# Score chunks in another order, first transposes earlier, norms spread out, last tile turned after one more half unit

## The chip, the cores and the metric

The kernel runs on one core of a Trainium2 chip. The metric is the device time of one execution, in microseconds. Inside a core TensorE (PE; weight loads are shown apart as PEld), VectorE (DVE), ScalarE (ACT) and GpSimd (POOL) each work through a queue of instructions in order and wait for each other through semaphores. SyncE (SP) issues most DMAs, in order; POOL and ACT issue some. SBUF is the on-chip memory, PSUM the banks that PE writes its products to.

## The reference

One transformer block on 2048 tokens of width 512, in float32: attention with 16 heads of 128, then a layer of 64 experts with 4 chosen for each token, plus shared experts.

```python
h = _layernorm(x) * (1 + ca) + sa
# attention, per head: q, k, v from h; causal softmax; out = sum over heads of attn @ O_w + O_b
logits = jnp.einsum('bqhd,bkhd->bhqk', q, k) / math.sqrt(d_head)
scores = jax.nn.softmax(jnp.where(causal_mask, NEG, logits), axis=-1)
out = jnp.einsum('bqhd,hdm->bqm', jnp.einsum('bhqk,bkhd->bqhd', scores, v), O_w) + O_b
x = x + ga * out
h = _layernorm(x) * (1 + cb) + sb
# router: softmax(h @ Wr + bias), top 4 of 64 experts, at most 128 tokens each
# experts: (silu(xb @ Wg) * (xb @ Wu)) @ Wd, weighted; shared experts: the same form on all tokens
x = x + gb * ffn(h)
```

`sa, ca, ga, sb, cb, gb` come from `silu(c) @ wmod`.

## The kernel before

The 2048 tokens are 16 tiles of 128. The order of the instructions is written by hand: the helper `merge` takes several streams of (cost, function) items and always emits the next item of the stream that is furthest behind by share of cost; *marks* are functions that are emitted when a given share of all cost is done. Within each engine instructions then run in the order in which they were emitted, apart from some products that are brought forward.

**Attention.** The query tiles are taken in pairs: pair `pr` is tiles 2pr and 2pr+1 (`i` = 0, 1). Causality gives tile qi a row of (qi+1)*128 columns of scores. A head is done in five steps s, with the pairs `BATCHES` = (7), (6), (5, 0), (4, 1), (3, 2). There are 80 steps (16 heads of five). In step n three things are merged: the softmax of step n+2, fillers (for s below 3 the projections of the next head's q and k by `project`, then the values of the next group of heads), and `weighted_values` of step n (scores times values, L644). The fourth thing is at the marks 0.58, 0.66, 0.8 and 0.88: the four transposes `turn(n + 1, a)` of step n+1.

A tile's row of scores is made in chunks of at most 1024 columns. For one chunk (`chunk`, in `softmax_tile`): PE writes the scores (L572) into one of **two** PSUM buffers `ps` (tag `sc`); DVE adds the causal mask to the last 128 columns (L584), finds the negated maximum (L585) and, for a second chunk, the minimum with the first (L589); ACT takes the exponential and the sum (L591) into `p`, and for a second chunk the factor `fix` (L601). When a tile has its last chunk, `normalise` is put on the list `left`; it is emitted inside the next chunk, or at the end of the step: L547 or L550 to L554 make the reciprocal sums. The scaling of `p` follows on ACT (L795) after the next chunk's exponential, or on DVE (L559) for tile 0 of the single pairs. A chunk's scores can start only when the exponential of the chunk two before has read its buffer.

At the end of each step `swap` issues 16 DMAs on SP (L616), 32 partitions by 32 columns blocks of `p` to `pt`; then DVE turns each of the four parts of `pt` in place (L626), and these are the right operands of L644. The four `turn`s of step 0 stand apart, ahead of the loop: steps 0 and 1 have their softmax before it, merged with the values of the first heads.

`project` makes seven products (L222) in two PSUM buffers of their own (tag `mm`): the first is read by ACT (L230), the second by DVE with the first's result (L236), the third by DVE (L240), the fourth by two (L248, L249), then L253, L257, L261.

`tiles_of(s)` gives the order of the tiles in a softmax step. Chunks of a tile are adjacent:

- (5, 0): (0,0) 128; (5,1) 1024, 512; (0,1) 256; (5,0) 1024, 384
- (4, 1): (4,1) 1024, 256; (1,1) 512; (4,0) 1024, 128; (1,0) 384
- (3, 2): (3,1) 1024; (2,1) 768; (3,0) 896; (2,0) 640

**Output tiles and routing.** The first `NE` = 4 output tiles have their first 15 heads done as fillers in attention's last steps; the last head is added at L1119 and L1126. Then `norm` is called for the four of them. `norm(t)` is seven instructions on DVE (L954 to L965), one square root on ACT (L958, before L959) and a DMA of h on POOL (L966). The tiles 4 to 15 follow, 16 heads of PE each (L1140). At places given by tables, `turn_h(t)` (four transposes on PE, L972, and a copy by ACT, L973), `logit(t)` (four products, L981), `choose`, `positions` and `seat_tokens` of earlier tiles are emitted between the heads: `turn_h(0)` after head 10 of tile 4, `logit(0)` after its head 14, `turn_h(1)` after head 0 of tile 5, `logit(1)` after its head 3. Two of PE's orders matter here: the buffer of the turned tile (tag `tr`) and the three instructions on ACT, root, copy and the exponential of `choose`, which share one queue.

**After the last tile** come the shared experts' first ten half units (`shared[:LEAD]`, eight PE instructions each, L1203; after two of them ACT and DVE make their gated product, L1191 to L1193), with the last tile's turn, seats, logit, choice and positions between them. Then the experts run, merged with the other shared units.

Of the kernel before, what the change touches and what calls it, by code (L numbers as in the profile page):

```python
# [23 lines left out]
def adaln_block_kernel(  # L24
# [24 lines left out]
    _, N, D = x.shape  # L49
    H, _, DH = Q_w.shape  # L50
    E, _, HE = Wg.shape
    S, _, HS = Sg.shape
# [68 lines left out]
    NE = 4  # L121
    parts = [silc.rearrange("p k n -> p (k n)")]
    with ExitStack() as att:
# [143 lines left out]
        with tc.tile_pool(name="pre", bufs=1) as pre, tc.manual_schedule():  # L267
# [4 lines left out]
            for b in range(NB):  # L272
# [5 lines left out]
                if b == 0:  # L278
                    wms = {}
                    for i in (1, 0):  # L280
                        wms[i] = pre.tile([P, DC, D], F32, name="wm", bufs=2)
                        nc.sync.dma_start(
                            out=wms[i],
# [233 lines left out]
                    return at  # L517
                at += 4 * o + 3

        def tiles_of(s):  # L520

            prs = BATCHES[s]
            if len(prs) == 1:
                return [(prs[0], 1), (prs[0], 0)]
            if prs[1] == 0:
                return [(0, 0), (prs[0], 1), (0, 1), (prs[0], 0)]
            return [(prs[0], 1), (prs[1], 1), (prs[0], 0), (prs[1], 0)]

        def softmax_tile(hd, s, pr, i, pb):

# [266 lines left out]
        probs = {}  # L797
        turned = {}

        def softmax_work(n):  # L800
            hd, s = steps[n]
            probs[n] = pp.tile([P, PW], F32, name="p")
            out = []
            for pr, i in tiles_of(s):
                out += softmax_tile(hd, s, pr, i, probs[n])
            return out

        def swap(n):
            flush()
# [3 lines left out]
        def turn(n, a):  # L813
            turn_blocks(steps[n][1], turned[n], a)

        with tc.manual_schedule():
            work = softmax_work(0) + softmax_work(1)
            fill = [(1024, lambda t=t: make_v(0, t)) for t in range(NT)]
            fill += [(2048, lambda j=j: plain(0, j, qts[0, j])) for j in (2, 0, 1)]
            merge([work[:4], fill[:8]], [])  # L820
            swap(0)
            merge([work[4:], fill[8:]], [])
            swap(1)
            for a in range(4):
                turn(0, a)
            outs = []
            for n, (hd, s) in enumerate(steps):
                if s == 3:
                    if hd + 2 < H:
                        heads[hd + 2] = load_head(hd + 2)  # L830
                    if hd % HG == 1 and hd // HG + 2 < NG:
                        groups[hd // HG + 2] = load_group(hd // HG + 2)
                fill = fillers(hd, s)
                if (hd, s) in MOD_LOADS:
                    load_mod(MOD_LOADS[hd, s], hd // HG)
                if (hd, s) in MOD_ROWS:
                    fill.append((2048, lambda m=MOD_ROWS[hd, s]: late_mod(*m)))
                if (hd, s) in ((2, 3), (15, 2)):
                    mag = qkw.tile([P, 512], F32, name="p_")
                    gate(mag, ga if hd == 2 else gb)  # L840
                if (hd, s) == (14, 0):
                    nc.sync.dma_start(out=sgb, in_=modd.partition_broadcast(P))
                if (hd, s) == (14, 1):
                    fill.insert(2, (0, lambda: load_wo(0)))
                if (hd, s) == (14, 2):
                    load_wo(1)
                    load_ab(0, heads=((0, 4), (4, 8)))
                if (hd, s) == (14, 3):
                    load_wo(2)
                    load_ab(0, heads=((8, 12), (12, 14)))  # L850
                    first, second = [
                        vow.tile([P, DC, HG, DH], F32, name="wv").rearrange("p k i d -> p (k i d)")
                        for _ in range(2)
                    ]
                    parts += [first[:, :D], first[:, D:], second[:, :D]]
                    last3 = second[:, D : D + (NE - 1) * P]
                if (hd, s) == (14, 4):
                    load_wo(3)
                    load_ab(0, heads=((14, 15),))
                    for u in range(NE):  # L860
                        load_x_tile(u)
                    rest = spare(hd // HG)
                    nc.sync.dma_start(out=rest[0][:, :D], in_=O_b.partition_broadcast(P))
                    for u in range(NE):
                        outs += begin_output(u)
                if hd == H - 1 and s == 0:
                    load_ab(1, heads=((0, 4), (4, 8)))
                if hd == H - 1 and s == 1:
                    load_ab(1, heads=((8, 12), (12, 15)))
                if hd == H - 1 and s == 2:  # L870
                    load_ab(2)
                if hd == H - 1 and s == 4:
                    nc.vector.tensor_copy(ga, rest[0][:, D:])
                    nc.sync.dma_start(out=last3, in_=atd[H - 1, :, : (NE - 1) * P])
                    nc.sync.dma_start(out=ones, in_=atd[H - 1, :, (NE - 1) * P : NE * P])
                if outs:
                    upto = 8 if hd < H - 1 else (14, 14, 14, 10)[s]
                    fill += outs[:upto]
                    del outs[:upto]
                streams = [fill, weighted_values(hd, s, turned.pop(n))]  # L880
                if n + 2 < len(steps):
                    streams.insert(0, softmax_work(n + 2))
                marks = [(f, lambda i=i: scale_wo(i)) for f, i in WO_SCALES.get((hd, s), ())]
                if s == 4 and hd + 2 < H:
                    marks.append((0.05, lambda: scale_w(hd + 2)))
                    marks.append((0.3, lambda: sum_w(hd + 2)))
                if n + 1 < len(steps):
                    for a, at in enumerate((0.58, 0.66, 0.8, 0.88)):
                        marks.append((at, lambda a=a: turn(n + 1, a)))
                merge([st for st in streams if st], marks)  # L890
                if n + 2 < len(steps):
                    swap(n + 2)
            assert not outs and not ahead
# [216 lines left out]
    with tc.manual_schedule():  # L1110
        load_x(1)
        load_ab(3, heads=ALL)
        load_ab(2, heads=((15, 16),))
        route_consts()
        for j in range(2, NB):
            load_x(j)
        for t in range(NE):
            ps = psO.tile([P, D], F32, name="pso", tag="y")
            nc.tensor.matmul(  # L1119
                out=ps,  # L1120
                lhsT=last3[:, t * P : (t + 1) * P] if t < NE - 1 else ones,
                rhs=wos[(H - 1) // 4][:, (H - 1) % 4, :],
                start=True,
                stop=True,
            )
            nc.vector.tensor_add(acc[:, t, :], parts[t], ps)  # L1126
        for t in range(NE):
            norm(t)
        for t in range(NE, NT):
            pr, i = divmod(t, 2)  # L1130
            if i == 0 and 3 <= pr < NP - 1:
                load_ab(pr + 1, heads=ALL)
            if i == 1 and pr >= NP - 1 - S:
                s = pr - (NP - 1 - S)
                if s < S:
                    nc.sync.dma_start(out=wsg[:, s], in_=Sg[s].rearrange("(k p) h -> p k h", p=P))
                    nc.sync.dma_start(out=wsu[:, s], in_=Su[s].rearrange("(k p) h -> p k h", p=P))
            ps = psO.tile([P, D], F32, name="pso", tag="y")
            for hd in range(H):
                nc.tensor.matmul(  # L1140
                    out=ps,
                    lhsT=abs_[pr][:, hd, i * P : (i + 1) * P],
                    rhs=wos[hd // 4][:, hd % 4, :],
                    start=(hd == 0),
                    stop=(hd == H - 1),
                )
                if hd == 5:
                    nc.vector.tensor_add(acc[:, t, :], acc[:, t, :], ga)
                if (t, hd) in TURN:
                    turn_h(TURN[t, hd])  # L1150
                if (t, hd) in POSITION:
                    positions(POSITION[t, hd])
                if (t, hd) in SEAT:
                    seat_tokens(SEAT[t, hd])
                if (t, hd) in LOGIT:
                    u = LOGIT[t, hd]
                    logit(u)
                    if u in LASTS:
                        for _ in choose(LASTS.index(u)):
                            pass  # L1160
            nc.vector.tensor_add(acc[:, t, :], acc[:, t, :], ps)
            norm(t)
# [3 lines left out]
    with ExitStack() as ex:  # L1166
# [214 lines left out]
        with tc.manual_schedule():  # L1381
# [3 lines left out]
                load_down(e)  # L1385
            for n, (_, f) in enumerate(shared[:LEAD]):
                f()
                if n == 1:
                    turn_h(NT - 1)
                if n == 2:  # L1390
                    seat_tokens(len(BLOCKS) - 2)
                if n == 2:
                    logit(NT - 1)
# [176 lines left out]
```

## Time and profile before

| | |
|---|---|
| runs, median (lowest to highest) | 2424.36 us (2423.91 to 2430.88) |
| the profiled execution | 2410.55 us, span 2408.8 |
| PE idle in the span (2408.8 - 2344.1) | 64.7 us |
| attention, start to the last weighted values | 54 to 1680 us |
| output tiles and routing | 1680 to 1884 us |
| shared first units | 1884 to about 1930 us |

A profile lists each engine's instructions by line of the kernel, with tiles as out<-in. "Idle before" is how long the engine stood still ahead of an instruction, and "<-" names what it waited for. The "granted clock" is the share of full speed that TensorE was given in a stretch. A matmul in float32 is issued as two instructions; 512 columns take 0.43 us each from start to start, 256 columns 0.215, although each is shown longer as they overlap. The 16 heads repeat with a period of about 97.5 us.

### The profile page before, as it was taken

How to read it: one execution, taken by the hardware profiler on the slowest of the kernel's cores; microseconds unless marked ns; L12 is line 12 of the kernel's file. 1: busy time of each engine (PE TensorE's matmuls, PEld its weight loads, DVE VectorE, ACT ScalarE, POOL GpSimd, SP SyncE). 2: the span in 40 equal slices, each digit the busy share in tenths (PEclk: the TensorE clock that was granted, in tenths of full speed). 3: DMA queues.
4: the chain of work that ended last, by engine and by line, in shares of the span. 5: the costliest groups of instructions: out<-in, count | busy, mean ns of one | idle time of the engine just before them, and what ended most of it. 6: DMA issues, size and time to landing. Idle time of an engine off the chain costs nothing.

```text
span 2408.8 us, 27742 instructions
## 1 busy us (share of the span) xinstructions
PE 2344.1 (97%) x9078; PEld 1503.7 (62%) x9078; DVE 1554.9 (65%) x3100; ACT 864.0 (36%) x1703; POOL 219.1 (9%) x286
## 2 busy tenths in 40 slices
PE   7999999999999999999999999999999999999999
PEld 3666656666576675766766656555444476876743
DVE  5367767677676776767767767764655563644664
ACT  3344444444444444444444444442211221222200
POOL 0000000000000000000000000000000111111074
PEclk9999999999999999999999999999999999999999
DMA  4234544354453444444535445675432368778665
GB/s 140 63 72 119 125 115 114 94 144 109 97 135 96 118 121 95 114 111 103 122 94 127 114 101 120 169 197 142 137 123 87 101 203 247 236 218 240 193 194 160
DMA packets 223835, 325.84 MB, mean 135 GB/s; under 512 B 31894, under 2 KB 138442, under 8 KB 223692
## 3 DMA queue, kind: packets, MB, share of 16 engines
q1 hardware_dynamic: 196812, 252.74, 40.8%
q0 software_dynamic: 17664, 54.54, 7.6%
q10 hardware_dynamic: 9216, 16.78, 1.9%
q8 instruction: 73, 1.20, 0.2%
q14 instruction: 70, 0.57, 0.1%
HBM read 139.39 MB, written 41.95 MB: 75 GB/s over the span
## 4 chain that ended last, share of the span: by engine, by line
PE 75%; SPq 7%; DVE 7%; issue 3%; DMA 3%; ACT 2%; POOL 1%; ACTq 0%; DVEq 0%
PE ps L572 14%; PE po L644 14%; PE pqk L222 14%; SPq L616 7%; PE pso L1140 6%; PE pst L1287 5%; PE pse L1432 5%; PE psd L1349 5%; PE pv L447 4%; DVE pt L626 3%; PE psy L1453 2%; PE psg L1203 2%; PE psb L769 2%; DVE nm L585 1%; PE tpx L1425 1%
## 5 line engine op out<-in xcount | busy, mean ns | idle before, releaser
L591 ACT ACTIVATE p<-ps,nm 128x1024 f32<-128x1024 f32 (+7 forms) x384 | 332.0, 865 | 872.4 <-DVE nm L589 422.4
L644 PE MATMUL po<-pt,v 128*128 128x256 f32 (+1 forms) x2304 | 565.0, 368 | 7.1 <-DVE pt L626 6.2
L644 PEld LDWEIGHTS po<-pt,v 128*128 128x128 f32 x2304 | 422.7, 190 | 221.9 <-issue 163.7
L572 PE MATMUL ps<-kt,qt 128*128 128x512 f32 (+3 forms) x1280 | 532.4, 532 | 28.2 <-ACT p L591 27.5
L585 DVE TENSOR_REDUCE nm<-ps 128x1 f32<-128x1024 f32 (+7 forms) x384 | 348.0, 909 | 76.0 <-PE ps L572 67.3
L626 DVE STREAM_TRANSPOSE pt<-pt 128x832 f32<-128x832 f32 (+2 forms) x320 | 338.6, 1071 | 22.3 <-DMA pt<-p 18.5
L572 PEld LDWEIGHTS ps<-kt,qt 128*128 128x128 f32 x1280 | 232.1, 191 | 189.3 <-issue 137.6
L795 ACT ACTIVATE p<-p,rs 128x1024 f32<-128x1024 f32 (+3 forms) x320 | 266.2, 860 | 6.5 <-DVE rs L554 6.3
L658 POOL DMA_DIRECT2D atd<-at x128 | 74.4, 585 | 1605.6 <-ACT at L653 1582.0
L1140 PE MATMUL pso<-hT,T 128*128 128x512 f32 x384 | 175.1, 601 | 0.0
L222 PE MATMUL pqk<-T,sw 128*128 128x512 f32 x360 | 169.2, 592 | 0.0
L584 DVE TENSOR_TENSOR ps<-ps,causal 128x128 f32<-128x128 f32 x256 | 73.4, 287 | 134.9 <-PE ps L572 133.3
L1432 PE MATMUL pse<-wgu,xbT 128*128 128x256 f32 x512 | 121.1, 379 | 0.0
L1140 PEld LDWEIGHTS pso<-hT,T 128*128 128x128 f32 x384 | 70.1, 192 | 72.1 <-issue 71.3
L222 PE MATMUL pqk<-hT,wq 128*128 128x512 f32 x240 | 112.8, 592 | 0.0
L1349 PE MATMUL psd<-wsd,hs 128*128 128x512 f32 x256 | 111.5, 592 | 0.0
L222 PEld LDWEIGHTS pqk<-T,sw 128*128 128x128 f32 x360 | 68.4, 190 | 54.1 <-issue 50.2
L1432 PEld LDWEIGHTS pse<-wgu,xbT 128*128 128x128 f32 x512 | 93.8, 190 | 11.7 <-issue 1.0
L1415 POOL DMA_INDIRECT xb<-h2d,tok x64 | 64.8, 1013 | 302.3 <-PE tpx L1425 275.5
L1427 ACT COPY xbT<-tpx 128x512 f32<-128x512 f32 x64 | 37.4, 586 | 146.0 <-DVE y L1455 56.5
L447 PEld LDWEIGHTS pv<-sgb,T 128*128 128x128 f32 x672 | 81.6, 192 | 8.1 <-issue 6.7
L1349 PEld LDWEIGHTS psd<-wsd,hs 128*128 128x128 f32 x256 | 48.6, 190 | 59.0 <-issue 58.1
(423 smaller groups left out, 2648.7 us busy)
## 6 DMA issues: line engine op xcount, KB each, us to landing
pt<-p SPq DMA_DIRECT2D x768, 104.0 KB, 2.2
pt<-p SPq DMA_DIRECT2D x256, 124.0 KB, 2.3
pt<-p SPq DMA_DIRECT2D x256, 108.0 KB, 2.2
atd<-at POOLq DMA_DIRECT2D x128, 128.0 KB, 2.2
wgu<-in_L_ffn_Wg_dram SPq DMA_DIRECT2D x64, 256.0 KB, 4.2
wgu<-in_L_ffn_Wu_dram SPq DMA_DIRECT2D x64, 256.0 KB, 5.0
wd<-in_L_ffn_Wd_dram SPq DMA_DIRECT2D x64, 256.0 KB, 4.1
ybd<-y ACTq DMA_DIRECT2D x64, 256.0 KB, 3.7
```

The source lines that it names most:

```text
L222: nc.tensor.matmul(out=ps, lhsT=l[:, k], rhs=r[:, k], start=(k == 0), stop=(k == 1))
L447: nc.tensor.matmul(out=ps[:, n], lhsT=l[:, k, n * P : (n + 1) * P], rhs=r[:, k], start=(k == 0), stop=(k == 1),)
L572: nc.tensor.matmul(out=ps[:, o : o + wo], lhsT=q, rhs=kts[hd, (c0 + o) // 512][:, :wo], start=True, stop=True,)
L585: nc.vector.tensor_reduce(nm[:, n : n + 1], ps[:, :w], AX.X, ALU.max, negate=True)
L591: nc.scalar.activation(rows[:, r0 + c0 // P : r0 + (c0 + w) // P], ps[:, :w].rearrange("q (r b k) -> q r b k", b=4, k=32), AF.Exp, bias=nm ...
L616: nc.sync.dma_start(out=pt[32 * b : 32 * (b + 1), a * w : (a + 1) * w], in_=pb[32 * a : 32 * (a + 1), b * w : (b + 1) * w],)
L626: nc.vector.transpose(part, part)
L644: nc.tensor.matmul(out=po if wide else po[:, P:], lhsT=vts[g, kt // 4][:, kt % 4, hh * DH : (hh + 1) * DH], rhs=rows[:, r : r + last + 1 : ...
L795: nc.scalar.activation(part, part, AF.Identity, scale=r)
L1140: nc.tensor.matmul(out=ps, lhsT=abs_[pr][:, hd, i * P : (i + 1) * P], rhs=wos[hd // 4][:, hd % 4, :], start=(hd == 0), stop=(hd == H - 1),)
L1349: nc.tensor.matmul(out=ps, lhsT=hsh[b, f][:, i * P : (i + 1) * P], rhs=wsd[:, f, :], start=(f == 0), stop=(f == NHC - 1),)
L1432: nc.tensor.matmul(out=ps, lhsT=xts[e][:, k, :], rhs=weights[e][:, k].rearrange("p i h -> p (i h)"), start=(k == 0), stop=(k == DC - 1),)
```

## The change

1. `tiles_of` is replaced by a table `CHUNKS` of (pair, tile, chunk), and `softmax_work` orders the chunks by it. The steps (7), (6) and (3, 2) keep their order. The two mixed steps get

   - (5, 0): (5,0) 1024; (0,0) 128; (5,0) 384; (5,1) 1024; (0,1) 256; (5,1) 512
   - (4, 1): (4,1) 1024, 256; (1,0) 384; (4,0) 1024, 128; (1,1) 512

2. The four transposes of step 0 become marks of the second merge before the loop.
3. Only `norm(0)` stays ahead of tile 4; norms 1, 2 and 3 are emitted within tile 4 after heads 10, 12 and 15.
4. `turn_h(15)` is emitted after the third half unit of the shared experts and no longer after the second, just ahead of the seats and the last logit.

```diff
-        def tiles_of(s):
...
+        CHUNKS = (
+            ((7, 1, 0), (7, 1, 1), (7, 0, 0), (7, 0, 1)),
+            ((6, 1, 0), (6, 1, 1), (6, 0, 0), (6, 0, 1)),
+            ((5, 0, 0), (0, 0, 0), (5, 0, 1), (5, 1, 0), (0, 1, 0), (5, 1, 1)),
+            ((4, 1, 0), (4, 1, 1), (1, 0, 0), (4, 0, 0), (4, 0, 1), (1, 1, 0)),
+            ((3, 1, 0), (2, 1, 0), (3, 0, 0), (2, 0, 0)),
+        )
...
-            out = []
-            for pr, i in tiles_of(s):
-                out += softmax_tile(hd, s, pr, i, probs[n])
-            return out
+            tiles = {}
+            for pr, i, _ in CHUNKS[s]:
+                if (pr, i) not in tiles:
+                    tiles[pr, i] = softmax_tile(hd, s, pr, i, probs[n])
+            assert sum(len(chunks) for chunks in tiles.values()) == len(CHUNKS[s])
+            return [tiles[pr, i][c] for pr, i, c in CHUNKS[s]]
...
-            merge([work[4:], fill[8:]], [])
+            marks = [(at, lambda a=a: turn(0, a)) for a, at in enumerate((0.55, 0.65, 0.75, 0.85))]
+            merge([work[4:], fill[8:]], marks)
             swap(1)
-            for a in range(4):
-                turn(0, a)
...
-        for t in range(NE):
-            norm(t)
+        norm(0)
...
+                if (t, hd) in ((4, 10), (4, 12), (4, 15)):
+                    norm({10: 1, 12: 2, 15: 3}[hd])
...
-                if n == 1:
+                if n == 2:
                     turn_h(NT - 1)
-                if n == 2:
                     seat_tokens(len(BLOCKS) - 2)
                 if n == 2:
                     logit(NT - 1)
```

More of the change, by code (lines that the diff above doesn't have):

```diff
@@ L518, in first_block @@
                 at += 4 * o + 3
-        def tiles_of(s):
[L522 to L527, printed above, removed]
+        CHUNKS = (
[5 rows of a table added]
+        )
         def softmax_tile(hd, s, pr, i, pb):
```

## The prediction

> **What bounds the kernel now.** I read the page's busy table first, then the list of who waited for whom on PE, then timelines around each of those waits, then clock windows. PE is busy 97% of the span, so only its waits and its slow stretches can be won.
>
> ```profile
> PE 2344.1 (97%) x9078; PEld 1503.7 (62%) x9078; DVE 1554.9 (65%) x3100; ACT 864.0 (36%) x1703; POOL 219.1 (9%) x286
> PE ps L572 <- ACT p L591: 27.5, 29, 1.5
> PE po L644 <- DVE pt L626: 6.2, 3, 3.5
> PE pl L981 <- ACT h2T L973: 4.5, 1, 4.5
> PE tp L972 <- DVE h L965: 3.3, 2, 3.0
> ```
>
> The last four lines (waited in total, times, longest) are what the four parts of the change lie at. The 29 score waits come in two kinds, one of each per head; head 1 shows both (start, length, idle before in brackets):
>
> ```profile
> 211.16 0.59 PE L644 MATMUL po<-pt,v 128*128 128x256 f32 x2
> 212.42 1.98 PE L572 MATMUL ps<-kt,qt 128*128 128x512 f32 x4 [0.67 <-ACT p L591]
> 214.25 1.46 PE L644 MATMUL po<-pt,v 128*128 128x256 f32 x6
> ...
> 249.29 0.75 DVE L240 SCALAR_TENSOR_TENSOR kt<-pqk,qkb,qt 128x512 f32<-128x512 f32 x1 [0.51 <-PE pqk L222]
> 249.95 1.03 DVE L626 STREAM_TRANSPOSE pt<-pt 128x832 f32<-128x832 f32 x1
> 251.73 0.37 ACT L591 ACTIVATE p<-ps,nm 128x128 f32<-128x128 f32 x1 [4.10 <-DVE nm L589]
> 252.24 1.98 PE L572 MATMUL ps<-kt,qt 128*128 128x512 f32 x4 [1.04 <-ACT p L591]
> ```
>
> A wait costs more than its bracket. At 212.42: the row before began at 211.16 and holds 0.43 us of issue, so PE was ready at 211.59; the waiting row then took 1.83 to the next row where an undisturbed one takes 1.72. That is 0.83 + 0.11 = 0.94, the bracket plus 0.27. Long waits also slow what follows (us, PE busy, ..., granted clock, DMA share, GB/s):
>
> ```profile
> 112.80:116.40 3.60, 3.52 (x6) 1.87 (x7) 0.51 (x3) 1.04 (x3) 0.00 (x0) 0.53 0.56 128
> 1702.30:1706.80 4.50, 4.48 (x12) 2.93 (x13) 2.73 (x5) 0.00 (x0) 0.54 (x1) 0.50 0.20 76
> 1891.40:1894.80 3.40, 3.31 (x8) 1.93 (x9) 0.00 (x0) 0.59 (x1) 0.54 (x1) 0.52 1.12 333
> 1571.00:1574.60 3.60, 3.48 (x12) 2.39 (x13) 3.15 (x8) 0.98 (x5) 1.28 (x2) 1.00 0.98 330
> ```
>
> After waits of 3.52, 4.47 and 2.98 us the clock is half for some 3.4 us or more; after 2.31 us it is not. So a wait of 3 us or more costs about 1.7 us on top.
>
> **Part 1, first transposes inside the second softmax: -5.5.** Now `turn(0, a)` for four blocks runs on DVE from 108.34 to 112.82, and the first weighted values wait for it:
>
> ```profile
> 107.47 1.88 PE L222 MATMUL pqk<-hT,wq 128*128 128x512 f32 x4
> 112.88 1.22 PE L644 MATMUL po<-pt,v 128*128 128x256 f32 x2 [3.52 <-DVE pt L626]
> 113.89 3.08 PE L572 MATMUL ps<-kt,qt 128*128 128x512 f32 x4
> ```
>
> In the new order of DVE's instructions the four stand between the reduces of step 1. DVE idles there (6.20 us before L584 at 104.02, 5.41 before 96.07), the swap's blocks have landed some 11 us after its start at 79.78, and the last transpose falls under the exp at 105.46 to 106.25, so no softmax row moves. PE then goes on from 109.19: its 0.43 + 1.72 would end at 111.34 instead of 116.81, 5.5 gained. Bounds: 3.8 if the clock were half anyway (3.52 + 0.27), 5.5 if not; I take 5.5.
>
> **Part 2a, the first score wait: -14.6.** There are two `sc` buffers, so a chunk waits for the exp of the chunk two before. Now the chunk of 128 goes first and the 1024 at 212.42 needs the buffer of (6,0)'s last 640 columns, whose exp ends at 212.28. New order: (5,0) 1024, (0,0) 128, (5,0) 384, (5,1) 1024, (0,1) 256, (5,1) 512. The 1024 needs a buffer that was read by 206.32: no wait. The 128 follows 1.72 (scores) + 1.72 (product) + 1.72 (four values) + 1.72 + 0.43 later, at 216.5, 4.2 after that exp. The 14 waits sum to 11.8 in brackets, with 0.27 each 15.6.
> What is late next: the 384 chunk at 217.2 needs the exp of the 1024. DVE is in the scalings of L559 until 214.46, reduces in 1.22, ACT takes 1.11: 216.8, only 0.3 ahead. In heads whose bracket is longer (1.52, 1.17, 1.05, 0.95 for 0.67) the excess over that slack comes back, 1.0 in all. ACT's L230 now stands behind the exp of 1024 and ends at 217.5 instead of 216.06; DVE's L236 and the third product (218.3, it needs that buffer) wait for it with 0.7 to spare.
>
> **Part 2b, the second score wait: -0.7, it stays.** The 1024 at 252.24 waits for the exp of (4,0)'s last 128 columns. In the new order that 128 is still the last but one of its step, so the same chain sets it: third product (starts 247.37), L240, the fourth transpose, causal add, reduce, exp; 252.24 - 247.37 = 4.87. What PE has to do meanwhile was 1.72 + 0.43 + 0.22 + 0.65 + 0.65 = 3.67 and becomes 1.72 + 0.22 + 0.43 + 0.86 + 0.65 = 3.88, as the chunk behind the 128 is 512 wide and no longer 384. So 0.21 less per head, 15 x 0.21 = 3.2.
> Against that, the swap of the (5,0) pair: its DMAs on SP start when ACT has scaled the last chunk, at 235.46 now. The last chunk becomes 512 (exp 0.69 for 0.58, scalings 1.76 for 1.65) with the 256's scaling (0.50) newly ahead of it. I put the start at 235.75, while PE comes about 1 us earlier. The third transpose needs the 15th of the 16 transfers, which in 11 heads lands about 11.0 after the start, so 246.8; DVE is ready for it at 246.85 (reduce of the 1024 from 243.0, two transposes, L236), so nothing is lost. In heads 1, 2, 7 and 14 one issue on SP took 1.4 to 1.8 instead of 0.64 and it landed at 11.7 to 12.2; there 0.4 to 0.9 is lost, 2.5 in all. Net 0.7. Bounds: swaps 1 us later than I lay them cost 15 x 0.8 = 12; a wait that is gone altogether brings 15 x 1.31 = 19.7. I stay near the rows.
>
> **Part 3, norms apart: -1.6.** Now ACT's copy of the first turned tile stands behind the four square roots, and the fourth of these behind four norms on DVE (3.38 us each, 1688.90 to 1703.76):
>
> ```profile
> 1701.31 0.30 ACT L958 ACTIVATE rstd<-mv,eps 128x1 f32<-128x1 f32 x1 [3.08 <-DVE mv L956]
> 1701.68 0.59 ACT L973 COPY h2T<-tp 128x512 f32<-128x512 f32 x1
> 1702.32 1.97 PE L981 MATMUL pl<-wr,h2T 128*128 128x64 f32 x8 [4.47 <-ACT h2T L973]
> 1710.28 1.00 PE L981 MATMUL pl<-wr,h2T 128*128 128x64 f32 x8
> ```
>
> After: the copy follows the first root, and the first logit runs at 1697.7 without a wait. But ACT's next rows are the roots of norms 1, 2, 3 and 4, and only then the copy of the second tile; the fifth root has norms 1 to 3, L1148 and L1161 ahead of it on DVE: 1693.62 + 0.73 + 3 x 3.38 + 0.73 + 0.94 = 1706.16, copy to 1706.95, second logit at 1707.0. PE would be there at 1703.27 (1698.53 after the first logit, two heads of 0.86, four transposes 0.44, three heads 2.58). The wait moves by one tile and is 3.6 us long, so half clock follows. Logit 1.7, the fifth head's product 1.7: the third turn at 1710.4, against 1712.03 now. 1.6 gained, where removing the wait alone looks like 7. Bounds: 0 (three norms later on DVE by a transfer) to 3.3.
>
> [...]
>
> **Part 4, last tile turned later: -4.3.** `turn_h(15)` waits 2.98 at 1891.49 for h, which DVE ends at 1891.34, held by the `hs` product of the first shared unit (L1193 at 1888.55). After, the half unit of 3.44 us (8 x 0.43) goes first: 1888.35 to 1891.79, h is ready, no wait and no half clock. Turn 0.44, seats 0.44, then the last logit waits some 0.4 for the copy (0.59 on ACT), as no product lies between them any more: it ends at 1893.95 against 1898.28. 4.3 gained; bounds 3.5 (copy late by an ACT table load, 1.28) to 4.7. All that follows in the shared and expert stages has no PE wait and keeps its distance.
>
> **Sum.** 5.5 + 14.6 + 0.7 + 1.6 + 4.3 = 26.7. The profiled execution took 2410.55 (span 2408.8 and 1.75 around it), so 2383.9 for one like it. The median of the runs shown is 2424.36, 13.8 above; I take the difference off that: 2397.7.
>
> **Rivals.**
> (a) The second wait grows: the later swap meets the earlier PE. For it: 0.05 us of slack at the third transpose. Against: it is a short overlap. At 1 us later the gain is 26.7 - 12 = 15, time 2409. Chance 0.20.
> (b) The same mechanism ending slower: swaps later by so much that the wait of 15 heads grows by over 1.8 each, 27 in all; from there slower. It needs the transfers over 2 us later than laid out, say 2.8: 15 x 2.6 = 39 against 27.4, time 2436. Only if DVE's queue in step 0 slips by several rows. 0.06.
> (c) The second wait goes altogether, because DVE gets its transposes done while PE is in the first 1024: 26.7 + 19, time 2379. The new DVE order, with L240 and a transpose still ahead of the 128, speaks against it. 0.12.
> (d) It moves waits only: the first wait reappears at the 384 chunk (0.3 slack), the logit wait costs what it did, leaving parts 1 and 4 less some loss: under 7 us, 2420. 0.08.
> Forecast: 0.54.
>
> **Numbers.** About 0.3% (7.3 us) is what a measurement of this kernel can tell from no change. Faster: 0.54 + 0.20 + 0.12 = 0.86; the same 0.08; slower 0.06. The range takes in the forecast, (a) and part of (c): 2384 to 2413.
>
> **What would show it.** PE's list of waits: po behind pt loses its 3.5; score waits fall from 29 to about 15, all at the chunk after the step with pair (4,1), about 1 us each; pl behind h2T has one wait of about 3.6 at the second logit with half clock behind it, and one of 0.4 at the last; tp behind h is gone. Wrong would be waits at the 384 chunk, transposes waiting for pt transfers in most heads, or a tp wait at 1891.

## The result, and the profile after

The changed kernel takes 2396.06 us in the median of four runs (2391.61 to 2400.6), the kernel before 2424.14 beside it (2420.91 to 2430.88): a ratio of 0.988, with a 95% interval of 0.9856 to 0.9904. Two later pairs on other occasions gave 0.9887 (0.9869 to 0.9904) and 0.9881 (0.9865 to 0.9898). The profiled execution took 2396.46, its span is 2394.7.

First the busy table of the page of the changed kernel, then its list of who waited for whom on PE (total, times, longest):

```profile
PE 2339.7 (98%) x9078; PEld 1504.3 (63%) x9078; DVE 1548.9 (65%) x3100; ACT 861.7 (36%) x1703; POOL 218.9 (9%) x286
```

```profile
PE ps L572 <- ACT p L591: 14.5, 16, 1.5
PE psg L1205 <- issue: 10.2, 1, 10.2
...
PE pl L982 <- ACT h2T L974: 3.4, 2, 3.2
PE po L644 <- DVE pt L626: 2.3, 1, 2.3
```

Of the four lines shown of before, the score waits fell from 29 to 16 and from 27.5 to 14.5 us, the first values' wait of 3.5 is gone, the logit wait is 3.2 where it was 4.5, and of the 3.3 us in which turned tiles waited for h one wait of 0.3 is left (the 3.0 at the last tile is gone). The second line is new: 10.2 us in the shared experts. PE's instructions around these places (start, length, idle before in brackets):

```profile
108.86 1.88 PE L222 MATMUL pqk<-hT,wq 128*128 128x512 f32 x4
110.58 1.89 PE L644 MATMUL po<-pt,v 128*128 128x256 f32 x8
...
147.37 0.82 PE L644 MATMUL po<-pt,v 128*128 128x256 f32 x4
149.02 1.98 PE L572 MATMUL ps<-kt,qt 128*128 128x512 f32 x4 [0.83 <-ACT p L591]
...
210.73 0.39 PE L572 MATMUL ps<-kt,qt 128*128 128x128 f32 x2
210.95 0.60 PE L644 MATMUL po<-pt,v 128*128 128x256 f32 x2
211.39 0.81 PE L572 MATMUL ps<-kt,qt 128*128 128x384 f32 x2
...
309.12 0.91 PE L572 MATMUL ps<-kt,qt 128*128 128x384 f32 x2 [0.66 <-ACT p L591]
...
1676.00 1.00 PE L982 MATMUL pl<-wr,h2T 128*128 128x64 f32 x8
...
1684.98 1.10 PE L982 MATMUL pl<-wr,h2T 128*128 128x64 f32 x8 [3.19 <-ACT h2T L974]
...
1869.55 1.10 PE L982 MATMUL pl<-wr,h2T 128*128 128x64 f32 x8 [0.23 <-ACT h2T L974]
...
2306.96 3.60 PE L1205 MATMUL psg<-h2T,wsg 128*128 128x512 f32 x8
2320.75 5.57 PE L1205 MATMUL psg<-h2T,wsu 128*128 128x512 f32 x8 [10.19 <-issue]
```

From the top: the first values follow the fillers without a gap (part 1). The wait at the step behind pair (4, 1) is 0.83 where it was 1.04. The chunks of 128 and 384 in the step of (5, 0) run without a wait in head 1, and in head 2 the 384 chunk waits 0.66, the only wait of the first kind that is left (those of the first kind stand at the start of the step of (5, 0), those of the second behind the step of (4, 1)). The first logit runs at once, the second waits 3.19 (part 3), the last 0.23 (part 4).

The span cut at marks that every run has on PE, in us: start to the first output projection of the last head (L1119 in the kernel before, L1120 in the changed one), from there to the third logit, from there to the end of the last logit, and from there to the end of the span. Here is the table, with all runs that follow:

| run | attention | to third logit | to last logit's end | shared and experts |
|---|---|---|---|---|
| before | 1680.35 | 42.27 | 175.83 | 510.3 |
| changed | 1658.77 | 40.34 | 171.55 | 524.0 |
| same_as_before | 1680.00 | 41.42 | 175.87 | 510.3 |
| old_chunk_order | 1675.10 | 41.56 | 171.55 | 511.6 |
| norms_behind_turn | 1657.12 | 38.91 | 171.55 | 510.7 |
| last_chunk_128 | 1641.86 | 41.16 | 171.56 | 510.7 |
| after_again | 1658.06 | 40.32 | 171.55 | 524.4 |
| turns_undone | 1664.23 | 42.24 | 171.56 | 523.7 |
| chunks_alone | 1662.15 | 42.72 | 175.97 | 524.2 |
| all_mended | 1640.63 | 35.98 | 171.56 | 523.7 |
| before_again | 1681.31 | 42.56 | 175.82 | 511.5 |
| after_third | 1661.62 | 41.93 | 171.54 | 511.5 |

In the first pair the three stages gave 21.6 + 1.9 + 4.3 = 27.8 us, and the last one took 13.7 back. That is why the two profiled spans differ by 14.1 only, while the medians differ by 28.1. ScalarE in the shared stage of the changed kernel shows where:

```profile
2269.39 0.60 ACT L1193 ACTIVATE sig<-psg 128x512 f32<-128x512 f32 x1 [2.35 <-PE psg L1205]
2319.37 0.60 ACT L1193 ACTIVATE sig<-psg 128x512 f32<-128x512 f32 x1 [49.39 <-remote]
```

The product that this sigmoid reads was on PE from 2300.09, and the next product started at 2303.52; in the kernel before the same sigmoid follows the one ahead of it after 33.74 us idle and not 49.39. PE ran on into its third `psg` buffer and then stood 10.19. Whether that belongs to the change had to be found out.

### The profile page after: what moved, and what is told of

Read it like the earlier page. It is cut to its first block, busy times and chain, and to the rows that moved or that the text cites. A ratio compares the mean times of both kernels' runs of the same rounds, so it can differ in the third digit from the quotient of the medians.

```text
span 2394.7 us, 27691 instructions
## 1 busy us (share of the span) xinstructions
PE 2339.7 (98%) x9078; PEld 1504.3 (63%) x9078; DVE 1548.9 (65%) x3100; ACT 861.7 (36%) x1703; POOL 218.9 (9%) x286
## 4 chain that ended last, share of the span: by engine, by line
PE 86%; DVE 4%; SPq 3%; issue 2%; ACT 1%; DMA 1%; DVEq 0%; ACTq 0%
PE po L644 17%; PE ps L572 17%; PE pqk L222 13%; PE pv L447 7%; PE pso L1140 6%; PE pst L1289 5%; PE pse L1433 5%; PE psd L1351 5%; PE psg L1205 3%; SPq L616 3%; PE psy L1454 2%; PE psb L769 2%; DVE pt L626 1%; PE tpx L1426 1%; PE pv L497 1%
## 5 line engine op out<-in xcount | busy, mean ns | idle before, releaser
L572 PE MATMUL ps<-kt,qt 128*128 128x512 f32 (+3 forms) x1280 | 532.2, 530 | 15.2 <-ACT p L591 14.5
L1433 PEld LDWEIGHTS pse<-wgu,xbT 128*128 128x128 f32 x512 | 93.8, 190 | 11.7 <-issue 1.0
```

The costliest lines, as they stand in the source:

```text
L572: nc.tensor.matmul(out=ps[:, o : o + wo], lhsT=q, rhs=kts[hd, (c0 + o) // 512][:, :wo], start=True, stop=True,)
L1433: nc.tensor.matmul(out=ps, lhsT=xts[e][:, k, :], rhs=weights[e][:, k].rearrange("p i h -> p (i h)"), start=(k == 0), stop=(k == DC - 1),)
```

## The experiments

### The kernel before against itself, and one part taken away at a time

`same_as_before` is the kernel before, unchanged. In `old_chunk_order` the two mixed steps of the changed kernel have the old order of the kernel before:

```diff
-            ((5, 0, 0), (0, 0, 0), (5, 0, 1), (5, 1, 0), (0, 1, 0), (5, 1, 1)),
-            ((4, 1, 0), (4, 1, 1), (1, 0, 0), (4, 0, 0), (4, 0, 1), (1, 1, 0)),
+            ((0, 0, 0), (5, 1, 0), (5, 1, 1), (0, 1, 0), (5, 0, 0), (5, 0, 1)),
+            ((4, 1, 0), (4, 1, 1), (1, 1, 0), (4, 0, 0), (4, 0, 1), (1, 0, 0)),
```

> The kernel before, unchanged, to see its last 500 us again. The profile shown of it took 2410.6 where its other executions took 2421 to 2431, and the changed kernel's profile holds one wait of 10 us (and half clock behind it) in the last stage, in which ACT stands still until a load of instructions has come. Theory: this late load is a matter of the single execution, and most executions of either kernel have it. Then this profile, if it is an ordinary one (2421 to 2431), has a stop of 10 to 15 us of ACT in the last 100 us and all else as before; the time from the end of the last logit to the end is about 524 us and no longer 510.6. Rival: the changed kernel's stop is its own (its transfers lie otherwise), and the 2421 to 2431 of before come from something spread over the kernel: then no stop here, and the stages up to the last logit are longer than 1898.3 us.

> The changed kernel with the old order of chunks; parts 1, 3 and 4 stay. Theory: the first weighted values start without a wait (part 1, 5.5 to 5.8), the 29 score waits of before are back (11.8 and 15.6 us in sum), attention ends 15 to 16 us later than in the changed kernel (last head's product about 1674 against 1658.8 us), the wait at the second logit (3.2 us) and the gain at the last tile (4.3) are as in the changed kernel. Rival: the four transposes inside the second softmax also made later waits shorter, so that less than 14 us come back.

The kernel before against itself: 2411.96 against 2412.78, a ratio of 1.0002 (0.9992 to 1.0011). So about 0.1% can be told apart here. The expectation of `same_as_before` could not be tested in this run: it needed an execution of 2421 to 2431, and here all of them lie near 2412, with no stop and a last stage of 510.3. `old_chunk_order`: 2401.91, ratio 0.9959 (0.9945 to 0.9973). Without the new order of chunks 10.9 us of the gain are left.

`norms_behind_turn`, below, has the changed kernel's attention and ran on the same chip. Between the two runs the attention ends at 1675.10 and 1657.12: the new order of chunks is worth 18.0 us, where 15 to 16 were expected. The sums of score waits are 27.8 us in 29 waits and 13.4 in 16. The brackets account for 14.4, and 13 waits less at 0.27 each for 3.5, together 17.9. The extra price of 0.27 that a wait has beside its bracket is borne out.

### The second score wait: the chunk of 128 last

`last_chunk_128` changes one row of the changed kernel's table. The 384 and the 512 of pair 1 both go ahead, so that the chunk of 128 is the step's last and the 1024 behind it takes the other buffer:

```diff
-            ((4, 1, 0), (4, 1, 1), (1, 0, 0), (4, 0, 0), (4, 0, 1), (1, 1, 0)),
+            ((4, 1, 0), (4, 1, 1), (1, 0, 0), (1, 1, 0), (4, 0, 0), (4, 0, 1)),
```

> The changed kernel with the step of pair (4,1) ordered (4,1) 1024, 256; (1,0) 384; (1,1) 512; (4,0) 1024, 128, so that the 128 columns are the last chunk and the next step's first chunk waits for the exp of (4,0)'s 1024. Theory (the second wait is set by the fourth transpose standing ahead of the 128 on DVE): the 15 waits of 0.83 to 1.46 us go, as that exp ends about 1.3 us before PE comes; attention ends 14.5 + 15 x 0.27 = 18 us earlier, about 1640 us. Rival (DVE as a whole is late there, or the swap's transfers): a wait of about the same size appears at another chunk of that step or the next, and attention ends within 4 us of the changed kernel's.

Measured: 2366.87, ratio 0.9813 (0.9797 to 0.983). PE in head 1 of this run:

```profile
242.75 0.38 PE L572 MATMUL ps<-kt,qt 128*128 128x128 f32 x2
242.97 0.39 PE L644 MATMUL po<-pt,v 128*128 128x128 f32 x2
243.19 1.88 PE L572 MATMUL ps<-kt,qt 128*128 128x512 f32 x4
```

and ACT at the exponential of that chunk of 128:

```profile
244.54 0.37 ACT L591 ACTIVATE p<-ps,nm 128x128 f32<-128x128 f32 x1 [1.95 <-DVE nm L589]
```

The 1024 now follows the 128 chunk without a bracket, although that chunk's exponential is still late: it starts 1.8 us after the chunk's scores and 1.35 us after PE has begun the 1024. All waits of the second kind are gone; two short ones of the first kind are left, 0.25 and 0.18. The wait was one for a buffer, as the prediction has it: not the DVE chain in itself, but that the chunk behind it needed the buffer at its end. The attention ends 15.3 earlier than in `norms_behind_turn`. The 13.4 of brackets with 0.27 each would be 17.7; what took the other 2.4 was not shown. The mean granted clock of the profiled execution is 0.997 here and 0.998 there, so one more stretch of half clock is the author's estimate for a part of it.

### The norms of the first tiles later

`norms_behind_turn` puts norms 2 and 3 behind the second turned tile, so that its copy on ACT stands ahead of their roots:

```diff
-                if (t, hd) in ((4, 10), (4, 12), (4, 15)):
-                    norm({10: 1, 12: 2, 15: 3}[hd])
+                if (t, hd) in ((4, 10), (5, 1), (5, 2)):
+                    norm({10: 1, 1: 2, 2: 3}[hd])
```

> The changed kernel with norms 2 and 3 emitted after heads 1 and 2 of tile 5, behind the second turn, so that the copy of the second turned tile on ACT stands behind two square roots fewer, and tile 4's norm on DVE ahead of norms 2 and 3. Theory: the second logit's wait of 3.2 us and the slow products behind it (the third turn at 1687.41, 28.4 us after tile 4's first head) go; the third turn comes 5 us earlier in the stage, and no later turn waits, since norm 2 ends about when PE gets there (within 0.5) and norm 3 two us ahead. Rival: the wait moves on to the third turn, whose h is now the last of the row on DVE: a wait of over 2 us there, and less than 2 us gained.

Measured: 2381.09, ratio 0.9876 (0.9859 to 0.9892). First ACT in the changed kernel, then PE and, in a fence of its own, DVE in this run:

```profile
1680.06 0.29 ACT L959 ACTIVATE rstd<-mv,eps 128x1 f32<-128x1 f32 x1 [3.09 <-DVE mv L957]
1684.16 0.29 ACT L959 ACTIVATE rstd<-mv,eps 128x1 f32<-128x1 f32 x1 [3.81 <-DVE mv L957]
1684.36 0.57 ACT L974 COPY h2T<-tp 128x512 f32<-128x512 f32 x1
```

```profile
1680.81 1.08 PE L1140 MATMUL pso<-hT,T 128*128 128x512 f32 x2
1684.02 1.09 PE L973 MATMUL tp<-ident,h 128*128 128x128 f32 x4 [2.13 <-DVE h L966]
1684.90 2.43 PE L1140 MATMUL pso<-hT,T 128*128 128x512 f32 x3
```

```profile
1679.80 0.69 DVE L966 TENSOR_TENSOR h<-h,sgb 128x512 f32<-128x512 f32 x1
...
1683.18 0.69 DVE L966 TENSOR_TENSOR h<-h,sgb 128x512 f32<-128x512 f32 x1
```

In the changed kernel the copy stands behind two more roots, each of which waits for a norm on DVE; the tile itself had been turned by 1679.2. With the norms later the second logit no longer waits, but the third tile to be turned does: its norm comes behind that of tile 4 (h at 1680.49) and ends at 1683.87. So the wait moved again, as the rival had it, and shrank to 2.13; the stage takes 38.91, 2.5 less than in the kernel before on that chip.

### The change once more, and its parts by themselves

These four ran on a chip on which the kernel before takes 2425.73 (2420.3 to 2429.53). `after_again` is the changed kernel. `turns_undone` has part 1 taken back, `chunks_alone` is the kernel before with part 2 alone, that is, the changed kernel with this and with parts 3 and 4 taken back as well:

```diff
-            marks = [(at, lambda a=a: turn(0, a)) for a, at in enumerate((0.55, 0.65, 0.75, 0.85))]
-            merge([work[4:], fill[8:]], marks)
+            merge([work[4:], fill[8:]], [])
             swap(1)
+            for a in range(4):
+                turn(0, a)
```

> The changed kernel once more, unchanged, beside the kernel before on the same chip. Two readings of the 13.3 us by which its shared stage ended late in its first profile (from the last logit's end to the span's end 524.0, against 510.3 before; ScalarE started the sigmoid at 2319.37 whose input was there at 2303.7). Theory: that stop is no part of the kernel; the stage takes 510 to 512, the first part up to the first output projection 1657 to 1659, span about 2381, time about 2384, ratio about 0.988. Rival: the stop comes with the kernel, because its instructions fall otherwise: the stage takes 524 again, time about 2397, ratio 0.993.

> The changed kernel with part 1 taken back: the first four transposes stand behind the second step's softmax again. Theory: the wait of 3.5 us before the first weighted values returns with half clock behind it, the attention ends 4.9 to 5.8 later than in the changed kernel, nothing else moves: about 2389. Rival (the wait was covered further on, part 1 is worth nothing by itself): the same time as the changed kernel, 2384.

> The kernel before with part 2 alone, the new order of chunks. Theory (the parts lie in stages that follow each other, so they add): score waits fall from about 28 us in 29 to about 13.5 in 16, and with 0.27 for each wait gone the attention ends 16 to 18 us earlier; the rest keeps its distances (41.4 from the first output projection to the third logit, 175.9 to the last, 510.3 to the end): time about 2395. Rival (the parts need each other): 5 us or more away from that.

`after_again`: 2396.59, ratio 0.9887 (0.9869 to 0.9904), last stage 524.4: the rival's time with the theory's ratio. `turns_undone`: 2403.72, 0.9897 (0.9872 to 0.9922). `chunks_alone`: 2406.68, 0.9921 (0.9897 to 0.9945), 11.7 above what was expected; its last stage too took 524.2, with the old norms, the old place of the last turn and the old start. So neither of parts 1, 3 and 4 is needed for those 13 us.

By the medians part 1 is worth 7.1 us inside the change and part 2 alone 19.1. The first figure holds more than part 1. Of the 6.2 us by which the attention of `turns_undone` ends later than that of `after_again`, 4.0 lie up to the first wait of the second kind (99.04 against 95.05 in the changed kernel's first profile, below) and 2.2 behind it; 1.9 more lie behind the second logit (42.24 for 40.32, with a granted clock of 0.50 over 6.0 us from 1690.7, and in `after_again` of 0.77, 0.50 and 0.76 over 1.0, 2.0 and 2.0 us from 1684.2). The 2.2 and the 1.9 are at places that the edit does not touch; the mean granted clock of the two executions is 0.993 and 0.995. And its own place shows two prices. In `chunks_alone` and `turns_undone` the first values wait 2.03 and not 3.52, the length that was expected for `turns_undone`, since the new order puts a chunk of 1024 on PE ahead of them in place of the one of 128. Clock windows over the 3.6 us from that point, of `chunks_alone`, `turns_undone` and, with the wait of 3.52, `same_as_before` (us, busy time and instructions of PE, PEld, DVE, ACT and POOL, granted clock, DMA share, GB/s):

```profile
112.70:116.30 3.60, 3.52 (x12) 2.39 (x13) 1.14 (x2) 1.78 (x3) 0.00 (x0) 1.00 0.60 139
```

```profile
113.40:117.00 3.60, 3.52 (x9) 2.81 (x10) 1.13 (x2) 1.78 (x3) 0.00 (x0) 0.54 0.66 152
```

```profile
113.30:116.90 3.60, 3.57 (x13) 2.41 (x14) 1.57 (x3) 1.03 (x3) 0.00 (x0) 1.00 0.55 125
```

The same wait of 2.03 was followed by full clock in one run and by half clock in the other, and the wait of 3.52, half clock in the first profile of the kernel before (0.53), left the clock at 1.00 here. From the first score row to the first wait of the second kind (149.02 in the changed kernel) it is 95.05 with part 1, 97.36 without it and with full clock, 99.04 without it and with half clock. With the old chunks it is 95.27 with part 1 (`old_chunk_order`), and 99.06 and 100.74 without it (`same_as_before` and the first profile). So part 1 brings 2.3 or 4.0 on top of part 2, and 3.8 or 5.5 without it.

### Both mends together

`all_mended` is the changed kernel with the row of `last_chunk_128` and with the norms so that the third comes ahead of the fifth:

```diff
-                if (t, hd) in ((4, 10), (4, 12), (4, 15)):
-                    norm({10: 1, 12: 2, 15: 3}[hd])
+                if (t, hd) in ((4, 10), (4, 12), (5, 2)):
+                    norm({10: 1, 12: 2, 2: 3}[hd])
```

> The changed kernel with the chunk of 128 of pair 1 ahead of the two chunks of (4,0), and with the second and third norm behind the tenth and twelfth head of output tile 4 and the fourth behind the second head of tile 5, so that the square root of the third norm comes before the copy of the second turned tile, and the third norm before the fifth. Theory: no score wait over 0.3 us in the heads and no wait at the second logit or at the third turn; from the first output projection to the third logit 35 us (41.4 before, 38.9 with the norms behind the turn), attention as in the run with the last chunk of 128 (end 1641.9): span 2359, time about 2361, ratio 0.979. Rival (the wait moves on once more, to the third or fourth turned tile): 38 to 40 us there, time 2364 to 2367.

Measured on the same chip as `after_again`: 2373.64, ratio 0.9787 (0.977 to 0.9803). It beats the kernel before by 52 us and the changed one by 23. PE from the second logit on:

```profile
1664.17 1.10 PE L982 MATMUL pl<-wr,h2T 128*128 128x64 f32 x8
1665.11 1.08 PE L1140 MATMUL pso<-hT,T 128*128 128x512 f32 x2
1666.02 0.60 PE L973 MATMUL tp<-ident,h 128*128 128x128 f32 x4
```

No wait at the second logit and none at the third turn; the stage takes 35.98, 4 to 6 less than with the norms as in the change. The first turn still waits 0.3. The ratio is as expected; the time is 13 above, because the 2361 had been reckoned from runs on a chip without the stop in the last stage.

### Whose are the 13 us in the last stage

`before_again` and `after_third` are the two kernels unchanged, one behind the other on a third chip.

> The kernel before once more, unchanged, for its own profile on the chip of the next run. Theory: the 13 us in the shared stage belong to the chip and not to a kernel. On a chip where the kernel before takes about 2425 its profile too shows the stage from the last logit's end at 523 to 526 instead of 510.3, with ScalarE or VectorE late behind a product that TensorE has long finished; on a chip where it takes about 2412 the stage is 510.3. Rival: the stop came with the new order of instructions; then the kernel before shows 510.3 wherever it runs.

> The changed kernel once more, unchanged, beside the run before it on the same chip. Theory: the three stages ahead of the last logit give 27 to 29 us on any chip, and the shared stage is as in the kernel before on that chip (within 2 us): ratio 0.988, about 2385 where the kernel before takes 2412, about 2397 where it takes 2425. Rival (the stop is the changed kernel's own): 2397 on a chip where the kernel before takes 2412, ratio 0.993. Half clock theory for the second logit (it starts where a window of some 3.4 us falls, not at the wait's end): from the first output projection to the third logit between 40.3 and 42.3, as the five runs so far, without a pattern.

The kernel before takes 2411.97 there (2412.5 as `before_again`, ratio 1.0002, 0.9993 to 1.0012), the changed kernel 2383.8: 0.9881 (0.9865 to 0.9898). The last stage takes 511.5 in both. ACT in `after_third`, at the sigmoid that stood 49.39 in the first profile:

```profile
2308.15 0.60 ACT L1193 ACTIVATE sig<-psg 128x512 f32<-128x512 f32 x1 [33.74 <-PE psg L1205]
```

So the changed kernel runs without the stop as well, and where the kernel before is 13 us slower the changed one is too: the gain is 28.2, 28.1 and 29.1 us in the three pairs. The stop goes with the chip, or with the occasion on which it was used, and not with the change. The expectations of `before_again` differ only for a chip on which the kernel before takes 2425, so that run could not decide between them. The kernel before was never profiled with the stop in it; that its own runs at 2424 and 2425 hold one is inferred from its 2412 elsewhere and from `chunks_alone`. What holds ScalarE back there the trace does not show. It is not shown to be the load of instructions that the expectation of `same_as_before` names: in the first profile one transfer of the profile's instruction queues starts at 2319.05, 0.3 us ahead of the late sigmoid, and takes 0.41, so that it ends behind the sigmoid's start, and in `after_again` it starts at 2318.17, behind the sigmoid at 2317.02. VectorE is late in the same place (an accumulation at 2306.01 after 8.83 us idle, put down to "remote", for a product whose last matmul PE started at 2299.66), so by the records both engines got late what PE had long done. No experiment was made on the cause; it stays open.

## Why the prediction was right, point by point

**The sum.** Forecast 2397.7, measured 2396.06, and 26.7 us of gain against 28.1. The sum was made for a profiled execution of 2410.55 and then lifted by 13.8 to the median. That lift held because, as far as the later pairs show, the 13 us are in both kernels on the chips concerned; the prediction had no account of the 13.8, so that part of 2397.7 was luck, and had the two been compared on different chips it would have been the largest error of all.

**Part 1, -5.5.** The first values now follow at once, and up to the first wait of the second kind 100.74 became 95.05, which is 5.7, of which 0.2 belong to part 2. Two things in the working were off. The wait would have been only 2.03 with part 2 alone, so the two parts overlap and the 5.5 are not part 1's own. And the half clock in it, 1.7, is not certain (3.8 without; the lower bound that was given).

**Part 2a, -14.6, and 2b, -0.7.** Together 15.3 forecast. In the first pair 21.6 less the 5.7 up to the first wait is 15.9, on the chip of the first experiments 18.0; the 15.9 is after 1.7 of half clock near 1550 (half of the 3.4 us from 1549.7), which the first profile of the kernel before has not (1.00 from 1571.0 to 1574.6, behind the same wait). The mechanism held: the first wait went in all heads but one, where the 384 chunk waits 0.66, as foreseen for the heads whose bracket was long (1.0 in all was set aside, 0.66 + 0.27 came). The second wait stayed, at 0.83, exactly the 0.21 less that were worked out from PE's work between. The swap in head 1 starts at 229.69; with the 5.8 by which head 0 ends earlier that is 235.49 in the time of before, where 235.75 was laid. In heads 1, 2, 7 and 14 the wait was longer, 1.46, 1.21, 0.92 and 1.08. What was mis-sized is the loss there: 2.5 were taken off, 0.63 + 0.38 + 0.09 + 0.25 = 1.4 were lost. Why these heads: in the trace of the changed kernel all 26 of the 1280 issues at L616 that took over 1 us lie within 0.5 us of the start of a transfer of 16 KB on queue q8, which its page lists as "instruction" (73 in the span). In head 1 the issue starts at 235.34 and the transfer at 235.37. In the kernel before the 27 issues over 1 us lie within 0.6 us of such a start too. That the load of instructions lengthens the issue was not tested.

**Part 3, -1.6.** The wait moved to the second logit as worked out, 3.19 long where 3.6 was forecast. In the first pair it brought 1.9. Over all runs the stage takes 42.27, 41.42, 42.56 and 42.72 with the old norms (mean 42.2) and 40.34, 40.32, 41.16, 41.56, 41.93 and 42.24 with the new (mean 41.3): 1.0 in the mean, between about 2 and none in single pairs. The step that failed is the rule behind it, "a wait of 3 us or more costs about 1.7 us on top".

That the first pair came near 1.6 was luck in part. The long wait of this stage was followed by half clock for one stretch of some 3.4 us in `same_as_before`, the changed kernel, `after_again` and `last_chunk_128` (granted clock 0.57 over 4 us from 1684.2 in `after_again`), and for a longer one, 6.8 us, in the first profile of the kernel before (from 1700.1), `old_chunk_order` and `after_third` (0.51 over 6.9 us from 1687.7 in `after_third`), and of at least 5.9, 5.6 and 6.0 us in `before_again`, `chunks_alone` and `turns_undone`, where the last window still shows 0.50. Among the first, 41.42 with the old norms stands against 40.34, 40.32 and 41.16 with the new, a gain of 0.8; among the second the means are 42.5 and 41.9, a gain of 0.6. The first pair set a long stretch against a short one. Windows in the changed kernel, from the second logit on:

```profile
1684.90:1685.90 1.00, 0.92 (x8) 0.92 (x9) 0.97 (x2) 0.98 (x2) 0.00 (x0) 1.00 0.00 0
1685.90:1687.90 2.00, 2.00 (x7) 0.99 (x7) 1.53 (x5) 0.64 (x2) 0.54 (x1) 0.59 0.00 0
1687.90:1689.90 2.00, 2.00 (x6) 1.12 (x5) 1.78 (x8) 0.59 (x1) 0.00 (x0) 0.56 0.35 131
```

and in `old_chunk_order`, where the same wait ended at 1701.31:

```profile
1696.00:1701.30 5.30, 2.12 (x5) 0.57 (x3) 4.33 (x11) 1.09 (x4) 0.90 (x2) 0.92 0.26 99
1701.30:1703.30 2.00, 2.00 (x9) 2.00 (x10) 1.64 (x3) 1.25 (x1) 0.00 (x0) 0.50 0.00 0
1703.30:1705.30 2.00, 2.00 (x4) 0.86 (x4) 1.51 (x7) 0.31 (x1) 0.54 (x1) 0.50 0.35 131
1705.30:1707.30 2.00, 2.00 (x6) 1.11 (x5) 1.79 (x6) 0.58 (x1) 0.00 (x0) 0.50 0.02 4
1707.30:1709.30 2.00, 2.00 (x6) 0.95 (x5) 1.69 (x6) 0.00 (x0) 0.00 (x0) 1.00 0.00 0
```

In the first the clock is full for a microsecond after the wait and then half; in the second it fell while PE still waited, some 0.85 us before its end (0.08 lacking of 1, doubled, times 5.3 us), and stayed at half until 1707.3, 6.8 us in all. PE stood still for the part in the wait, and what is left behind it is put at half its length, an estimate from these windows: 1.7 us in the first run and 3.0 in the second. The stages of the two, 40.34 and 41.56, differ by 1.2.

**Part 4, -4.3.** About 4.3 in every run that has it: 175.82 to 175.97 became 171.54 to 171.56. The last logit waits 0.23 for the copy, 0.4 was forecast, and no half clock follows in the changed kernel's first profile (1.00 over 4.0 us from 1869.5).

**The rivals.** The second wait did not grow beyond four heads (a, b), nor did it go (c); `last_chunk_128` shows what it takes for that, and it is the case that (c) priced at 19, though not by the way that (c) gave: the chunk of 128 is still late, but the 1024 behind it no longer needs its buffer. Of (d), which had the first wait reappear at the 384 chunk, one head in sixteen was seen.

## What to carry to other kernels

With two buffers in turn, ask of each item not only how long its own chain is but which item needs that buffer next: a short item with a long chain belongs where the one behind it takes the other buffer, and moving one row of a table was worth 15 us here. On an engine with one queue, a cheap instruction that waits held up what stood behind it: here a square root of 0.29 us stood 3.81 for its norm and ran at 1684.16, and the copy of a tile turned by 1679.2 came at 1684.36. So norms are to be emitted in the order in which their results are needed and behind the copies that are already due. Cut two profiles at common marks before comparing their totals: the stages gave 27.8 us where the spans differed by 14.1.

## What the runs showed of the hardware

**Half clock comes by phase.** After the same wait of 3.52 us the granted clock was 0.53, 1.00 and 0.56 in three runs of one program; after 2.03 us it was 1.00 and 0.54. At a wait near 1548, of 2.33 us in the changed kernel and 2.48 in `norms_behind_turn`, the shorter one was followed by half clock, the longer not. Windows from the end of that wait, of the changed kernel:

```profile
1548.40:1550.40 2.00, 1.90 (x6) 1.39 (x7) 1.55 (x6) 0.93 (x4) 0.77 (x2) 0.83 1.07 373
1550.40:1552.40 2.00, 2.00 (x5) 1.20 (x5) 2.00 (x3) 0.45 (x1) 0.51 (x1) 0.50 0.68 213
1552.40:1554.40 2.00, 2.00 (x6) 1.04 (x5) 0.72 (x2) 0.76 (x2) 0.00 (x0) 0.82 0.93 204
```

and of `norms_behind_turn`, where the clock is 1.00 in the windows before and behind as well, from 1548.4 to 1556.4:

```profile
1550.40:1552.40 2.00, 2.00 (x8) 1.29 (x7) 2.00 (x3) 0.41 (x1) 0.54 (x1) 1.00 0.90 270
```

Both profiles of the first pair have the clock at 1.00 or at 0.50 and at nothing between; then the time at half is twice what the clock lacks of 1, times the window: 0.68 + 2.0 + 0.72 = 3.4 us in the first, and 1.64 + 1.76 = 3.4 behind the second logit. So stretches of half clock were 3.4 us long in both places, and 6.8, twice that, behind the second logit of `old_chunk_order`, with starts that bore no fixed distance to the wait. Within a profile the starts keep a beat: in the changed kernel's first one half clock starts at 1549.71, 1686.25 and 2314.30 (0.82 over 2 us from 2313.0), so 136.5 and 628.1 us apart, 40 and 184 times 3.413; in that of the kernel before at 112.89, 1700.09 and 1891.24, 465 and 56 times that. The length of the wait alone did not decide it: waits of 2.03, 2.13 (granted clock 0.57 from 1683.0 to 1687.0 in `norms_behind_turn`) and 2.33 us came with half clock, where 2.98 was the shortest that did in the first profile of the kernel before.

**On some occasions one stage alone is slower.** On two occasions of four the kernel before took 2424 to 2426 and on two 2412; where changed kernels were profiled on the slower ones, all of the 13 us stood in the last stage (523.7 to 524.4 us, against 510.3 to 511.6), at one sigmoid and the rows behind it, while the changed attention ended at 1658.1 in `after_again`, and at 1657.1 (`norms_behind_turn`) and 1661.6 (`after_third`) on the two others.
